# Normalizing two groups of the second batch beside the first batch's products

## The chip, the cores and the metric

The kernel runs on one core of one Trainium2 chip. The metric is the device time of one execution in microseconds (us); lower is better.

## The reference

The input x is 128 samples of 128 nodes with 256 features, adj is 128 matrices of 128x128; everything is float32. Two layers follow each other, each added to its input:

```
h = relu(layernorm(x));  x = x + L0(h, adj)
h = relu(layernorm(x));  x = x + L1(h, adj)
```

L0 computes a convolution branch (a 1x1 convolution, relu, a convolution of 17 taps over the nodes, relu with a skip), a neighbour branch (a 3-component embedding, A = exp(-distance) * adj, and A times a message product), and combines both with h in a GRU cell. L1 is a small graph network: five groups of up to 25 nodes, two graph convolutions each, weighted and added.

## The kernel before

The 128 samples are worked on in 32 groups (q) of 4, and for the convolution in two batches of 16 groups. The 17-tap convolution is done in the frequency domain, with 80 points and 40 frequency steps (f from 0 to NF = 39).

The stages that matter here:

- `stage_a(q)` (L367): loads x of a group into a tile xa, takes mean and variance (`moments`, L261: per group four bn_stats, four bn_aggr and one add on VectorE, then a power on POOL, which is GpSimd), normalizes in place (`normalize`, L273: four tensor_scalar on VectorE), transposes on TensorE into PSUM (ph, L386), copies with relu to hTa on ScalarE, sends hTa to memory for later (L391), multiplies by the 1x1 convolution (pc, L397; its bias add is h, L400), and transforms to frequencies (pf, L408) into the big tile X.
- `stage_b(bat)` (L477): the products of one batch. For each f, two weight planes are loaded ahead (wf, L487, on SP's queue, into one of four buffers), POOL adds two pairs of operands (xs L495 and wf L496), TensorE makes pa and pb (L501), ScalarE copies pb to kk, VectorE combines them to y (L524), and POOL sends y to memory (yd).
- `early(q)` (L632): the neighbour branch of a group, five kinds of TensorE work (pse L580, pm L600, pd L613 with the turn of adj L615, px L626) with VectorE and ScalarE between them (ef, lr, msg, aT, xnmp). It is independent of the products, and is run beside stage_a and stage_b.
- `fold_gates` (L304): loads the gate weights on SP, then combines them in place on POOL (wrz, wn, wh).
- Later, `stage_c` (the inverse transform and the GRU cell) and the second layer, which the change does not touch.

The instructions' order is written by a planner in Python, not by the hardware. Each stage is a generator that emits some instructions and yields (cost, latency): the planner's clock advances by the cost, and this generator is not asked again before the latency has passed. A `Lane` is a list of generators of which up to `ahead` run at once; `Order.run` (L183) always asks the lane with the least work done per weight among those that are ready. A step of no cost raises its lane's account to the least of the others. On the chip each engine then runs its own queue strictly in the order emitted.

In this order, the first batch's stage_a ends and its products run beside `early`; then `take_turn` closes the pool of the products (xw) and opens that of stage_a (ab) in the same memory, and stage_a of groups 16 to 31 starts, three groups ahead, beside `early` and `fold_gates`. Where a tile of the new pool lies on one of the old pool, its first writer waits for that tile's last reader. In stage_a, a group that is not yet loaded is loaded by its own stage, with a planned pause of 6 us for the first group of a batch and 14 us for the others; the following group is loaded too, without a pause. Statistics and normalize follow, with pauses of 3 and 2 us:

```
for n in range(q, min(q + 2, (q // BQ + 1) * BQ)):
    if n not in XA:
        load_xa(n)
        if n == q:
            yield 0.0, 14.0 if q > BQ else 6.0
```

PSUM (the memory that TensorE writes) is divided into three buffers with the tag gat and five with the tag tmp; ph, pc, pf, pb, pse, pm, pd and px all take theirs from tmp.

Of the kernel before, what the change touches and what calls it, by code (L numbers as in the profile page):

```python
# [9 lines left out]
FP = mybir.dt.float32  # L10
# [5 lines left out]
B, N, D = 128, 128, 256  # L16
# [3 lines left out]
P = 128  # L20
# [7 lines left out]
BQ = BG // GB  # L28
# [179 lines left out]
def kernel(ctx: ExitStack, tc: tile.TileContext, x, adj, consts, vecs, w_se, conv1_w,  # L208
# [24 lines left out]
    def c(name):  # L233
        a, b = CAT[name]
        return cst[:, a:b]
# [25 lines left out]
    def moments(src, tag):  # L261

        st = f2.tile([P, 4, 6], FP, tag=tag + "st", name="st", bufs=4)
        mv = f2.tile([P, 4, 2], FP, tag=tag + "mv", name="mv", bufs=4)
        rs = f2.tile([P, 4], FP, tag=tag + "rs", name="rs", bufs=4)
        for t in range(4):
            nc.vector.bn_stats(st[:, t], src[:, t])
            nc.vector.bn_aggr(mv[:, t], st[:, t])
        nc.vector.tensor_scalar(rs, mv[:, :, 1], EPS, None, op0=ALU.add)
        nc.gpsimd.tensor_tensor(rs, rs, c("mhalf")[:, :4], ALU.pow)  # L270
        return mv, rs

    def normalize(dst, src, mv, rs):  # L273
        for t in range(4):
            nc.vector.tensor_scalar(dst[:, t], src[:, t], mv[:, t, 0:1], rs[:, t:t + 1],
                                    op0=ALU.subtract, op1=ALU.mult)
# [27 lines left out]
    def fold_gates():  # L304

        wrz, wn, wh = LATE["wrz"], LATE["wn"], LATE["wh"]
        x_in = w_ih.rearrange("(a k p) o -> k p a o", a=2, k=2)
        for slot, (i, k) in ((0, (0, 0)), (1, (0, 1)), (3, (1, 1)), (4, (1, 0))):  # L310
            nc.sync.dma_start(out=wrz[:, slot, 0],
                              in_=w_hh[k * P:(k + 1) * P, i * D:(i + 1) * D])
            nc.sync.dma_start(out=wrz[:, slot, 1:], in_=x_in[k, :, :, i * D:(i + 1) * D])
            nc.sync.dma_start(out=wn[:, slot],
                              in_=x_in[k, :, :, 2 * D + i * P:2 * D + (i + 1) * P])
            nc.sync.dma_start(out=wh[:, slot, 0], in_=w_hh[k * P:(k + 1) * P,
                                                           2 * D + i * P:2 * D + (i + 1) * P])
            yield 0.0, 8.0
        for w in (wrz, wn, wh):
            for dst, a, b, op in ((6, 0, 4, ALU.subtract), (4, 4, 3, ALU.add),  # L320
                                  (5, 4, 0, ALU.subtract), (2, 1, 5, ALU.subtract)):
                nc.gpsimd.tensor_tensor(w[:, dst], w[:, a], w[:, b], op)
                yield 0.0, 5.0
            nc.gpsimd.tensor_scalar(w[:, 3], w[:, 3], -1.0, None, op0=ALU.mult)
            yield 0.0, 5.0
# [16 lines left out]
    lab, turn = ExitStack(), []  # L342
    xf = lab.enter_context(tc.tile_pool(name="xf", bufs=1, side="right"))
    X = xf.tile([P, 2, F, P], FP, name="X")
    c1w = xf.tile([P, 2, D], FP, name="c1w")
    brow = xf.tile([P, D], FP, name="brow")
    LATE, XA, MOM = {}, {}, {}
    A_DONE, B_DONE, G_DONE, C_DONE = set(), set(), {-1}, set()

    def take_turn(name, bufs, **kw):  # L350
        while turn:
            turn.pop().close()
        turn.append(ExitStack())
        LATE[name] = turn[-1].enter_context(
            tc.tile_pool(name=name, bufs=bufs, side="right", **kw))

    def load_x(t, q):
        for j in range(GB):
            nc.sync.dma_start(out=t[j * WIDE:(j + 1) * WIDE],
                              in_=x[q * GB + j].rearrange("(t n) c -> n t c", n=WIDE))  # L360

    def load_xa(q):
        if q not in XA:
            XA[q] = LATE["ab"].tile([P, 4, D], FP, tag="xa", name=f"xa{q}", bufs=4)
            load_x(XA[q], q)

    def stage_a(q):  # L367
        ab = LATE["ab"]
# [5 lines that stand above are left out]
# [103 lines left out]
    def stage_b(bat):  # L477
        while "wrz" not in LATE:
            yield 0.0, 0.5
        if bat == 0:  # L480
            yield 0.0, 10.0
        WF, xf = {}, LATE["xw"]

        def load_w(f):
            w = WF[f] = xf.tile([P, 2, 3, D], FP, tag="wf", name=f"wf{bat}_{f}", bufs=4)
            for k in range(2):
                nc.sync.dma_start(out=w[:, k, :2], in_=wfd[f::NF + 1, k * P:(k + 1) * P]  # L487
                                  .rearrange("s p o -> p s o"))

        XS = {}  # L490

        def add(f):

            XS[f] = xf.tile([P, 2, P], FP, tag="xs", name=f"xs{bat}_{f}", bufs=2)
            nc.gpsimd.tensor_tensor(XS[f], X[:, :, 2 * f], X[:, :, 2 * f + 1], ALU.add)  # L495
            nc.gpsimd.tensor_tensor(WF[f][:, :, 2], WF[f][:, :, 0], WF[f][:, :, 1], ALU.add)  # L496

        def product(ps, xk, f, s):

            for k in range(2):  # L500
                nc.tensor.matmul(ps, xk(k), WF[f][:, k, s], start=(k == 0), stop=(k == 1))  # L501

        for f in range(3):
            load_w(f)
        yield 0.0, 5.0
        late = None
        for f in range(NF + 1):
            if f + 3 <= NF:
                load_w(f + 3)
            if f < NF:  # L510
                add(f + 1)
            y = xf.tile([P, 2, D], FP, tag="y", name=f"y{bat}_{f}")
            pa = pgat.tile([P, 2, D], FP, tag="gat", name=f"pa{bat}_{f}")
            for s in range(2):
                product(pa[:, s], lambda k: X[:, k, 2 * f + (s if f == 0 else 1 - s)], f, s)
            if f == 0:
                nc.vector.tensor_copy(y, pa)
            else:
                pb = ptmp.tile([P, D], FP, tag="tmp", name=f"pb{bat}_{f}")
                xs = XS.pop(f)  # L520
                product(pb, lambda k: xs[:, k], f, 2)
                kk = xf.tile([P, D], FP, tag="kk", name=f"kk{bat}_{f}", bufs=2)
                nc.scalar.activation(kk, pb, AF.Copy)  # L523
                nc.vector.scalar_tensor_tensor(y, pa, 2.0, kk[:, None].to_broadcast([P, 2, D]),  # L524
                                               op0=ALU.mult, op1=ALU.subtract)
            WF.pop(f)
            if late is not None:
                nc.gpsimd.dma_start(out=yd[bat][:, 2 * f - 2:2 * f], in_=late)
            late = y
            yield 1.7 if f == 0 else 2.6, 1.0  # L530
        nc.gpsimd.dma_start(out=yd[bat][:, F - 2:F], in_=late)
        B_DONE.add(bat)
# [99 lines left out]
    def early(q):  # L632

        while q not in A_DONE:
            yield 0.0, 0.5
        if q not in EN:
            EN[q] = load_n(q)
            yield 0.0, 6.0
        hT, ad = EN.pop(q)
        if q + 1 < NQ and q + 1 in A_DONE:  # L640
            EN[q + 1] = load_n(q + 1)
        xm = LATE["fr"].tile([P, 2, 512], FP, tag="xnmp", name=f"xnmp{q}", bufs=2)
        yield from neighbours(q, hT, ad, xm)
        nc.gpsimd.dma_start(out=xmd[q], in_=xm)
        E_DONE.add(q)
# [447 lines left out]
    order = Order()  # L1093
    take_turn("ab", 2)
    load_xa(0)
    nc.scalar.dma_start(out=c1w, in_=conv1_w.rearrange("(k p) o -> p k o", p=P))
    load_xa(1)
    load_taps(0, nc.sync, nc.gpsimd, nc.scalar)
    load_xa(2)
    fold()  # L1100
    beside = Lane([tap_weights()] + [early(q) for q in range(NQ)])
    gates = Lane([fold_gates()], weight=0.5)
    for bat, (during_a, during_b) in enumerate(((0.66, 0.5), (0.2, 0.65))):
        if bat:
            take_turn("ab", 2, reuse_waits="tile")
        begin = Lane([stage_a(q) for q in range(bat * BQ, (bat + 1) * BQ)], ahead=3)
        beside.weight = during_a
        order.run(begin, beside, *[gates] * bat, until=begin)
        take_turn("xw", 3, reuse_waits="tile")
        products = Lane([stage_b(bat)])  # L1110
        beside.weight = during_b
        order.run(products, beside, *[gates] * bat, until=products)
    turn.pop().close()
    lab.close()
    LATE["co"] = ctx.enter_context(
# [48 lines left out]
```

## Time and profile before

| | us |
|---|---|
| three runs: lowest, median, highest | 2123.21, 2127.03, 2128.71 |
| profiled execution: its own time | 2123.83 |
| its span, first to last instruction | 2122.0 |
| stage_a of the first batch and tap weights | 0 to 209.5 |
| products of the first batch | 209.5 to 369 |
| stage_a of the second batch | 369 to about 536 |
| products of the second batch | about 536 to 703.5 |
| stage_c and the second layer | to 2122 |

The profile is that of one execution. Its engines are PE (TensorE; PEld is its weight load), DVE (VectorE), ACT (ScalarE), POOL (GpSimd) and SP, which here only issues DMAs. A row of a stretch gives its begin and end, its length, then for PE, PEld, DVE, ACT and POOL the busy time and the number of instructions, then the granted TensorE clock (1 is full), the mean busy share of the 16 DMA engines, and GB/s. A row of a timeline gives start, duration, engine, line, operation, tiles and shape; in brackets stands how long the engine was idle just before, and what it waited for. L386 is line 386 of the kernel.

### The profile page before, as it was taken

Reading aid. Unit: us, or ns where it says so; the run is one execution under the profiler, and the core shown is the slowest. Engines: PE = TensorE matmul, PEld = TensorE weight load, DVE = VectorE, ACT = ScalarE, POOL = GpSimd, SP = SyncE. Lnnn points to the kernel's source line nnn. Section 1 sums busy time; section 2 is a strip of 40 time slices with the busy share of each in tenths; the row PEclk is TensorE's granted clock in tenths of the full one; section 3 lists DMA queues with packets and bytes.
Section 4 is the critical chain, followed back from the end, with each engine's and each line's share of the span. In section 5 each row is a group of like instructions: output and inputs, shape, how many; then the busy total and the mean of one; then the engine's idle time right before and its main releaser. Section 6 shows DMA issues by size and latency. Waiting matters only on the chain.

```text
span 2122.0 us, 31227 instructions
## 1 busy us (share of the span) xinstructions
PE 2050.2 (97%) x11316; PEld 1663.0 (78%) x11316; DVE 1239.7 (58%) x2999; ACT 699.6 (33%) x1575; POOL 723.3 (34%) x900
## 2 busy tenths in 40 slices
PE   6999999999999999999999999999999999999998
PEld 4667888788888777788778778878887887878875
DVE  5665444776544566746654655666565655665642
ACT  3554222344222343333223332232223323323333
POOL 2433665331565123512322233223323323233230
PEclk9999999999999999999999999999999999999999
DMA  9997878744787535222223232223232333223121
GB/s 180 270 265 231 261 255 266 217 144 145 256 262 257 171 110 162 61 90 69 69 70 103 77 82 81 78 81 80 75 94 73 81 92 88 78 80 101 26 78 50
DMA packets 187053, 281.68 MB, mean 133 GB/s; under 512 B 20686, under 2 KB 140243, under 8 KB 186899
## 3 DMA queue, kind: packets, MB, share of 16 engines
q1 hardware_dynamic: 156066, 184.81, 30.3%
q0 software_dynamic: 30000, 94.13, 13.9%
q8 instruction: 90, 1.47, 0.3%
q10 hardware_dynamic: 832, 0.74, 0.2%
q14 instruction: 65, 0.52, 0.1%
HBM read 187.34 MB, written 92.27 MB: 132 GB/s over the span
## 4 chain that ended last, share of the span: by engine, by line
PE 84%; DVE 8%; DMA 4%; ACT 2%; issue 1%; POOL 1%; SPq 0%; ACTq 0%; DVEq 0%; POOLq 0%
PE p L708 36%; PE pa L501 7%; PE pm L600 5%; PE ph L1024 5%; PE pz L1033 5%; PE pc L397 4%; PE pb L501 3%; PE px L626 3%; PE pi L673 3%; PE pf L408 2%; PE pg L1067 1%; PE po L848 1%; PE pc L687 1%; DMA xa<-in_x 1%; DMA wfd<-ws 1%; PE py L1007 1%
## 5 line engine op out<-in xcount | busy, mean ns | idle before, releaser
L828 POOL TENSOR_TENSOR d<-hTc,r 128x512 f32<-128x512 f32 x64 | 82.3, 1287 | 318.2 <-ACT r L825 307.8
L857 POOL DMA_DIRECT2D out<-xt x128 | 71.8, 566 | 263.0 <-DVE xt L854 259.0
L501 PE MATMUL pa<-wf,X 128*128 128x256 f32 x640 | 152.4, 381 | 0.0
L524 DVE SCALAR_TENSOR_TENSOR y<-pa,kk 128x512 f32<-128x512 f32 x78 | 53.8, 689 | 147.4 <-ACT kk L523 147.4
L722 ACT ACTIVATE r<-r,brz 128x256 f32<-128x256 f32 x128 | 58.1, 500 | 226.2 <-DVE r L769 198.5
L708 PE MATMUL p<-th,wrz 128*128 128x256 f32 x512 | 131.5, 379 | 0.7 <-ACT u L740 0.7
L708 PE MATMUL p<-tc,wrz 128*128 128x256 f32 x512 | 131.5, 379 | 0.4 <-DVE tc L552 0.4
L708 PE MATMUL p<-tm,wrz 128*128 128x256 f32 x512 | 131.4, 379 | 0.0
L501 PEld LDWEIGHTS pa<-wf,X 128*128 128x128 f32 x640 | 118.1, 190 | 16.4 <-issue 2.2
L397 PE MATMUL pc<-c1w,hTa 128*128 128x256 f32 x512 | 122.8, 386 | 3.5 <-ACT ef L588 2.3
L600 PE MATMUL pm<-wmsg,hT 128*128 128x256 f32 x512 | 123.3, 386 | 0.0
L690 DVE SCALAR_TENSOR_TENSOR xc<-pc,s_bn,hTc 128x256 f32<-128x256 f32 x128 | 53.1, 477 | 115.6 <-PE pc L687 115.6
L1024 PE MATMUL ph<-yz,w 128*128 128x96 f32 (+3 forms) x640 | 114.8, 334 | 4.0 <-DVE ve L795 2.7
L1024 PEld LDWEIGHTS ph<-yz,w 128*128 128x128 f32 x640 | 92.6, 202 | 26.0 <-issue 15.0
L397 PEld LDWEIGHTS pc<-c1w,hTa 128*128 128x128 f32 x512 | 94.3, 192 | 21.8 <-DVE h L400 4.0
L600 PEld LDWEIGHTS pm<-wmsg,hT 128*128 128x128 f32 x512 | 96.9, 192 | 16.3 <-issue 1.4
L1033 PE MATMUL pz<-hh,w 128*128 128x96 f32 (+3 forms) x640 | 108.6, 322 | 0.8 <-ACT hh L1026 0.8
L708 PEld LDWEIGHTS p<-th,wrz 128*128 128x128 f32 x512 | 97.2, 190 | 14.3 <-ACT u L740 1.1
L708 PEld LDWEIGHTS p<-tc,wrz 128*128 128x128 f32 x512 | 97.2, 190 | 14.0 <-DVE tc L552 0.8
L708 PEld LDWEIGHTS p<-tm,wrz 128*128 128x128 f32 x512 | 97.3, 190 | 13.2
L722 ACT ACTIVATE z<-z,brz 128x256 f32<-128x256 f32 x128 | 58.1, 501 | 145.7 <-DVE z L780 90.9
L1033 PEld LDWEIGHTS pz<-hh,w 128*128 128x128 f32 x640 | 87.3, 192 | 19.3 <-ACT hh L1026 1.5
(209 smaller groups left out, 4664.5 us busy)
## 6 DMA issues: line engine op xcount, KB each, us to landing
wf<-wfd SPq DMA_DIRECT2D x160, 256.0 KB, 3.8
wfd<-ws POOLq DMA_DIRECT2D x64, 320.0 KB, 7.2
yd<-y POOLq DMA_DIRECT2D x80, 256.0 KB, 3.9
yt<-yd SPq DMA_DIRECT2D x64, 320.0 KB, 4.5
w<-in_W SPq DMA_DIRECT2D x40, 512.0 KB, 3.6
xa<-in_x SPq DMA_DIRECT2D x128, 128.0 KB, 4.9
hTd<-hTa POOLq DMA_DIRECT2D x32, 512.0 KB, 4.7
hT<-hTd SPq DMA_DIRECT2D x32, 512.0 KB
```

The costliest lines, as they stand in the source:

```text
L397: nc.tensor.matmul(pc[:, i], hT[:, k, (2 * h + i) * N:(2 * h + i + 1) * N], c1w[:, k], start=(k == 0), stop=(k == 1))
L501: nc.tensor.matmul(ps, xk(k), WF[f][:, k, s], start=(k == 0), stop=(k == 1))
L524: nc.vector.scalar_tensor_tensor(y, pa, 2.0, kk[:, None].to_broadcast([P, 2, D]), op0=ALU.mult, op1=ALU.subtract)
L600: nc.tensor.matmul(pm[:, i], hT[:, k, j * N:(j + 1) * N], LATE["wmsg"][:, k], start=(k == 0), stop=(k == 1))
L626: nc.tensor.matmul(px[:, dc, i], msgs[h][:, i, dc * P:(dc + 1) * P], aT[:, 2 * h + i], start=True, stop=True)
L673: nc.tensor.matmul(pi[b * 64:(b + 1) * 64], inv[:F], yt[:, b::2], start=True, stop=True)
L708: nc.tensor.matmul(ps[:, m], w[:, i, k, m * P:(m + 1) * P], factor(i, x, t), start=first and j == 0, stop=last and j == len(n) - 1)
L722: nc.scalar.activation(dst[:, m], src[:, m], AF.Sigmoid, bias=brz[:, b + m:b + m + 1])
L828: nc.gpsimd.tensor_sub(d, hT[:, dc], r[:, dc])
L857: nc.gpsimd.dma_start(out=out[q * GB + j, WIDE:].rearrange("(t n) c -> n t c", n=WIDE), in_=xt[j * WIDE:(j + 1) * WIDE, 1:4])
L1024: nc.tensor.matmul(ph, w1[:, k, m * P:(m + 1) * P], yz[:, k, :, o:o + n], start=(k == 0), stop=(k == 1))
L1033: nc.tensor.matmul(pz, w2[:, g, m, cc * P:(cc + 1) * P], hs[g][:, m], start=(m == 0), stop=(m == 3))
```

## The change

A pool xe with two tiles of its own is opened beside X. While the first batch's products run, a third lane holds one generator, `first_of(1)`: it waits until the products have come to step f = 26, loads x of groups 16 and 17 into the two tiles, and after a planned pause of 14 us takes the moments of the one, normalizes it, and then does the same with the other. stage_a of groups 16 and 17 then finds XA and MOM filled and begins with the transposes. The other groups' tiles still come from the pool ab. In the second batch's products the lanes are as before.

```diff
+    xe = lab.enter_context(tc.tile_pool(name="xe", bufs=1, side="right"))
...
+    def first_of(bat):
+
+        while LATE.get("f", 0) < 26:
+            yield 0.0, 0.5
+        for q in (bat * BQ, bat * BQ + 1):
+            XA[q] = xe.tile([P, 4, D], FP, name=f"xa{q}")
+            load_x(XA[q], q)
+        yield 0.0, 14.0
+        for q in (bat * BQ, bat * BQ + 1):
+            MOM[q] = moments(XA[q], "a")
+            yield 0.0, 4.0
+            normalize(XA[q], XA[q], *MOM[q])
+            yield 0.0, 4.0
...
         for f in range(NF + 1):
+            LATE["f"] = f
...
         beside.weight = during_b
-        order.run(products, beside, *[gates] * bat, until=products)
+        order.run(products, beside, gates if bat else Lane([first_of(1)]), until=products)
```

## The prediction

> **What bounds the kernel now.** I read the page first, then the busy time of each engine by stage, then TensorE's timeline across the seam between the batches, and last the other engines there.
>
> ```profile
> PE 2050.2 (97%) x11316; PEld 1663.0 (78%) x11316; DVE 1239.7 (58%) x2999; ACT 699.6 (33%) x1575; POOL 723.3 (34%) x900
> PE 84%; DVE 8%; DMA 4%; ACT 2%; issue 1%; POOL 1%; SPq 0%; ACTq 0%; DVEq 0%; POOLq 0%
> 209.50:369.00 159.50, 159.50 (x958) 137.99 (x956) 75.94 (x130) 39.12 (x104) 99.13 (x123) 1.00 0.78 256
> 369.00:397.00 28.00, 23.39 (x155) 18.23 (x153) 20.98 (x64) 7.49 (x20) 5.27 (x7) 0.94 0.95 278
> 397.00:420.00 23.00, 23.00 (x148) 20.88 (x148) 17.64 (x50) 10.86 (x25) 7.80 (x8) 1.00 0.45 134
> 420.00:442.00 22.00, 19.10 (x127) 16.53 (x126) 18.15 (x42) 10.83 (x25) 10.83 (x10) 1.00 0.37 120
> ```
>
> TensorE (the first number after each stretch's length) is busy 97% of the span; all its idle time together is 72 us, so a change that removes no TensorE work can only win there. The rows are the first batch's products (209.5 to 369), the seam (369 to 397) and the start of the second batch's stage_a. In the products TensorE never stops and VectorE (the third busy time) works 75.9 of 159.5 us. At the seam TensorE stands still 4.6 us, its clock falls to 0.94, and VectorE works 21.0 of 28 us. The timeline of TensorE shows what it does there:
>
> ```profile
> 371.29 2.05 PE L626 MATMUL px<-aT,msg 128*128 128x128 f32 x16 [0.91 <-DVE aT L618]
> 379.32 0.48 PE L613 MATMUL pd<-lr 32*128 32x128 f32 x2 [1.33 <-DVE msg L603]
> 380.34 2.06 PE L386 MATMUL ph<-cst,xa 128*128 128x128 f32 x8
> 382.20 3.33 PE L626 MATMUL px<-aT,msg 128*128 128x128 f32 x16
> 391.83 1.69 PE L386 MATMUL ph<-cst,xa 128*128 128x128 f32 x8 [0.34 <-PE pm L600]
> 395.84 0.81 PE L408 MATMUL pf<-cst,h 128*128 128x160 f32 x4 [1.78 <-ACT ef L588]
> 396.90 1.35 PE L408 MATMUL pf<-cst,h 128*128 128x160 f32 x8 [0.25 <-DVE msg L603]
> ```
>
> The first transposes of group 16 (ph) start at 380.34, 11 us after the last product; until then TensorE runs `early` work, a filler that it can do anywhere. Idle time understates the loss, since ph goes at the pace of normalize (8 in 1.86 us from start to start; 0.87 where x is ready, 401.67 to 402.54) and px at a slow clock (16 in 3.17 us). So I price 369.29 to 396.90 by start-to-start times in undisturbed stretches: 16 pd 0.88, 8 adj turns 0.98, 32 px 3.56, 32 pse 1.14, 24 pm 5.16, 16 ph 1.74, 16 pc 3.46, 8 pf 1.09: 18.0 us of work in 27.6. **The seam loses 9.6 us**, 0.45% of the time; that is what the change can reach. The next stretch loses nothing. A later one (420 to 442, 2.9 us idle) is another matter:
>
> ```profile
> 420.92 5.20 DVE L275 TENSOR_SCALAR xa<-xa,mv,rs 128x256 f32<-128x256 f32 x4
> ```
>
> Four normalizes, elsewhere 0.40 us each, take 5.20 us while POOL adds wrz (1.83 us each, L322).
>
> **What the Trainium skill says.** "SBUF — State Buffer", section "Who interferes with whom": VectorE in a two-port mode, which tensor_scalar can enter, and GpSimd share a port pair as an exclusive lock, and the loser waits for a whole instruction. The 5.20 us agrees. "DMA: Bandwidth & Descriptors", section "Issuing engines are not separate DMA queues": all DMAs run on the same 16 engines and interleave. The trace agrees in that wf loads land in 4.1 us (median, 300 to 370) at a share near 0.8, and a 256 KB wrz load in 8.8 us at 0.95. "TensorE: Matmul & The Clock Gate", section "What's actually happening": the clock falls after an idle window of about 3.4 us. Here it fell to 0.83 (380 to 390) with no gap over 1.33 us, so I don't count on the page for it.
>
> **The change, part by part.**
>
> 1. Added beside the products: 8 DMAs of 128 KB on SP. first_of polls after step f=26. Steps come every 3.9 us and f=36 began at 352.8, so this is about 314. Price: 8 x 0.43 = 3.4 us of SP, and 1 MB at the 260 GB/s of the stage, 4 us of the DMA engines. Behind them on SP stand the next wf load and the early loads. A wf tile is loaded three steps (11.7 us) ahead of its product and two (7.8 us) ahead of POOL's add, and lands in 4.1 us; if late by 3 to 7 us it delays the add by 0 to 3.5, and pb needs the sum 3 us after the add's usual end. Cost to TensorE: 0 to 3 us, taken as 0. The new pool is written by nothing before, so these loads wait for no tile. More traffic speeds nothing up, so a gain is excluded.
> 2. Added on VectorE in 313 to 367: per group 4 statistics at 0.40, 4 aggregates at 0.18, one add at 0.17, 4 normalizes at 0.40: 4.1 us, 8.2 us for both, into 29 us that it idles there (25.05 of 54 busy). If POOL's adds (xs 0.74, wf 1.27) stretch both normalize blocks to the 5.2 us seen above, 15.4 us: still inside. What is queued behind a block decides: y has two further PSUM buffers and 7 us, msg and lr more. The aT products have little: pd at 331.9, aT done at 333.97, px at 335.43, 1.5 us to spare. A 2.5 us block of moments ahead of aT costs TensorE about 1 us. By the planned times (14.0 after a load at f=26, steps 3.7 apart with a beside step between) the first block falls behind f=30, just ahead of such a pd. The others fall beside px, pse and pm. POOL gets two pows of 1.03 us, as much less later. Cost: 0 to 4 us; I take 0.7.
> 3. Moved away from the seam: the same 8.2 us of VectorE, 2 pows, 8 DMAs. Group 16's and 17's transposes can follow the last product (pm ends about 369.2) at once, and stage_a skips its planned waits of 6, 14, 3 and 2 us. Early work is filler, so the two cycles that stood there are done later where TensorE is full anyway: no gain and no cost by themselves.
> 4. What is late next. (a) PSUM: the tag tmp has five buffers; after ph of group 16 (two), pd wants four, and ph of group 17 two more, each freed through ScalarE and VectorE: about 2 us. (b) stage_a(17) loads group 18, and stage_a(18), started right after it, issues moments(18) with no planned wait: the 14 us pause was only for a group that a stage loads itself. VectorE is one queue; h1 of group 16, msg and xnmp stand behind that wait. Before, group 18's DMAs went out at 367.70, freed by the last pb, and landed in 2.7 us, so by 372.2; VectorE would come to them about 374. No wait, if the tile lies where it did. (c) Group 19's loads went out from 375.47 and landed in up to 7.3 us, by 387; its moments come when group 16 is done, about 383: 0 to 4 us. Together I leave 4 us of loss at the seam (bounds 2 and 13).
> 5. The planner. The new lane keeps `products` from being credited while it waits at its start. Products then lead over beside by more, but each step's pause of 1.0 already admits one beside step, the order that the timeline shows: no change. After the seam about 11 us of early work slides to later, and with it the phases at 703 to 730, where TensorE idles 3.3 of 26.5 us, and POOL's wrz adds against normalize: -2 to +2 us, taken as 0.
>
> **Sum.** 9.6 - 4 - 0.7 = 4.9 us less: the profiled execution's 2123.83 (span 2122.0 and 1.8 around it) becomes 2118.9. It lies 3.2 us under the median of the three runs, 2127.03, and is no different program; from the median I forecast **2122.0 us**. 0.3%, or 6.4 us, is about what a measurement of this kernel can tell from no change, so the forecast lies just inside it.
>
> **Rivals.**
>
> - *Fuller gain.* The filler covers the PSUM turns, loss left 1 to 2 us, and the relieved VectorE also escapes the stretch at 420 (half of 2.9): 8 to 10 us, 2118. For it: 397 to 420 loses nothing at nearly the same mixture. Against: five buffers.
> - *Gain handed back.* The moved filler is missed or bunches at another stage start, or the products lose 3 us: 0 +- 3, 2126. For it: 703 to 730 loses as at the seam.
> - *Slower: moments(18) blocks VectorE.* If group 18's tile lies where group 19's did (375.47), landing by 387, VectorE stands from 374 to 387 with h1 of group 16 behind it. TensorE has transposes, pc and px for about 9 us, until PSUM is full at 383, and then waits out the landing, 2.6 us of moments and the backlog, 9 to 12 us; with 4 us of other loss that is 13 to 16 against 9.6, and with up to 3 us in the products +4 to +9: 2133.5. It decides from a landing after about 384. Against it: group 18 is the first tile of its tag, and the earlier ones were free by 367.7.
> - *The change doesn't do what it says.* The 30 planned us of first_of must fit before the products end: 13 steps remain, 48 us. Excluded.
>
> **How the numbers follow.** Likeliest case 45% (2119 to 2124), fuller gain 25%, handed back 15%, slower 15%. Faster by over 0.3% takes the fuller gain and a third of the likeliest: 0.40; slower takes most of its case: 0.14; the rest 0.46. The range from 2114.5 to 2130 leaves out the far slower half and the best tail.
>
> **What would show it.** Right: ph starts within 2 us of the last product; the products stay 159 to 161 us long; bn_stats of group 18 doesn't wait for its DMA; the seam's TensorE idle falls from 4.6 to under 2 us; `early` ends later. Wrong: DMA xa as the releaser of statistics near 374, px waiting for aT by several us at 330 to 345, wf late for POOL, or a longer idle at 703 to 730.

## The result: slower, and where the profile shows it

| | before, us | after, us |
|---|---|---|
| runs of the comparison: lowest, median, highest (4 each) | 2118.18, 2125.12, 2128.71 | 2146.71, 2151.92, 2152.57 |
| span of the profiled execution | 2122.0 | 2149.4 |

After takes 1.0118 times as long as before, 95% interval 1.0097 to 1.0138. The forecast was 2122.0 (2114.5 to 2130): neither its range nor its sign held. The line numbers of after are 15 or 16 higher than those of before from line 367 on (L626 has become L642, L708 L724); each row has those of its own kernel.

The page of after, row of busy time. TensorE issues the same 11,316 matmuls but is busy 17.5 us longer, and it stands still for 81.7 us where it was 71.8. So most of the 27.4 us that the span has gained is TensorE working slowly, not standing still:

```profile
PE 2067.7 (96%) x11316; PEld 1673.5 (78%) x11316; DVE 1242.3 (58%) x2999; ACT 706.1 (33%) x1579; POOL 722.4 (34%) x900
```

The stretches that the prediction showed, now of after:

```profile
209.50:369.00 159.50, 156.00 (x931) 133.72 (x930) 83.56 (x152) 37.47 (x101) 99.82 (x124) 0.99 0.79 254
369.00:397.00 28.00, 27.37 (x177) 24.37 (x176) 14.61 (x34) 12.03 (x27) 5.50 (x9) 1.00 0.88 262
397.00:420.00 23.00, 20.18 (x114) 17.20 (x112) 14.25 (x47) 7.92 (x17) 3.12 (x4) 0.85 0.52 148
420.00:442.00 22.00, 20.70 (x122) 18.26 (x115) 18.25 (x44) 9.28 (x22) 11.93 (x10) 0.96 0.31 109
```

The products (first row) now contain 3.5 us of idle TensorE where there was none. The seam (second row; in after its first 5 us still belong to the products, which end at 374.3 instead of 367.6) is what was hoped for: idle 0.6 us instead of 4.6, clock 1.00 instead of 0.94. The row after it had lost nothing before; now it idles 2.8 us at a clock of 0.85. The matmul counts in the same 28 and 23 us say so too: 155 and 148 before, 177 and 114 after.

The largest loss is in none of these rows. It lies 480 us later, in stage_c, which the diff does not touch. First before, then after:

```profile
880.00:930.00 50.00, 50.00 (x229) 38.52 (x225) 28.61 (x70) 15.04 (x35) 15.89 (x22) 0.97 0.23 65
```

```profile
880.00:930.00 50.00, 42.27 (x176) 32.60 (x175) 32.55 (x87) 11.82 (x24) 22.50 (x37) 0.83 0.27 72
```

**A measure for the whole run.** Stages shift against each other, so equal times are not equal work. I give each matmul record a price: the mean of the shorter nine tenths of the distances from start to start between neighbours of its kind (same tiles and shape) in before. Lost time of a part is the time it took less the prices of the matmuls in it. It counts idle time and slow clock together. Its own bias shows in the second batch's products, which never stop and "lose" 7.6 to 8.9 us in every kernel. Every "lost" is read from one execution; kernels of one and the same order differ by 1 to 2 us in a part, and by up to 4 us in the first. In us:

| part (ends with) | before | after | difference |
|---|---|---|---|
| up to the first batch's last pb | 82.1 | 88.8 | +6.7 |
| stage_a of the second batch (last pf) | 18.4 | 19.9 | +1.5 |
| products of the second batch | 8.5 | 8.3 | -0.2 |
| to the first matmul of stage_c (pi) | 6.5 | 6.7 | +0.2 |
| stage_c to the second layer's block 0, then block 1 (their pdg) | 10.9, 2.5 | 27.8, 3.9 | +18.3 |
| rest | 73.6 | 74.5 | +0.9 |
| sum | 202.5 | 229.9 | +27.4 |

The sum is the difference of the spans. There are three things to explain: 18.3 us in stage_c, 6.7 us up to the end of the products (0.8 of them before the first product, where nothing was changed), and a stage_a that gained 9 us at its start and kept none of it.

**The 18.3 us.** stage_a of the two groups no longer has its planned pauses for statistics and normalize, and the planner puts one cycle of `early` less beside stage_a and one less beside the products that follow: 16 cycles are done when stage_a ends (17 before), 27 when stage_c starts (29 before). With the loads alone moved, as in a kernel below, 17 and 29 stay. The rest is done beside stage_c, and the second layer's `setup_1` (L880) begins only after all of it (`while len(E_DONE) < NQ: yield 0.0, 1.0`, L881). The last cycle's pse moves from 800.9 to 833.6, and with it pb2, a matmul near the end of `setup_1`, from 851.8 to 876.5. After `setup_1`, `prepare(blk)` (L949) then lets POOL add adjacency rows into b (L961), VectorE sum them to dg (L966), and TensorE multiply both (pa, pdg). This is where it now falls, all engines of after in order of start (start, duration, engine, line, operation, tiles):

```profile
889.07 0.59 PE L724 MATMUL p<-tc,wn 128*128 128x256 f32 x2
...
891.24 0.15 DVE L940 TENSOR_SCALAR rs<-mv 128x1 f32<-128x1 f32 x1
891.54 0.55 POOL L941 TENSOR_TENSOR rs<-rs,cst 128x1 f32<-128x1 f32 x1 [6.14 <-DVE rs L940]
892.07 2.93 POOL L961 TENSOR_TENSOR b<-aj,cst 25x400 f32<-25x400 f32 x8
893.06 0.77 DVE L966 TENSOR_REDUCE dg<-b 25x16 f32<-25x400 f32 x2 [1.67 <-POOL b L961]
...
895.03 0.25 DVE L966 TENSOR_REDUCE dg<-b 25x16 f32<-25x96 f32 x1 [0.26 <-POOL b L961]
895.21 0.40 DVE L823 TENSOR_TENSOR v<-v,p 128x256 f32<-128x256 f32 x1
...
895.66 1.22 PE L724 MATMUL p<-tm,wn 128*128 128x256 f32 x2 [6.00 <-DVE v L823]
896.67 1.06 PE L724 MATMUL p<-tc,wn 128*128 128x256 f32 x2
```

Read the brackets from the bottom up. TensorE stood 6.00 us for v. v (L823) stood in VectorE's queue behind the sums (L966). The sums stood for POOL's b. POOL could not begin b until its power (L941) was done, for which it had waited 6.14 us for VectorE. Every engine was idle in turn. Afterwards two matmuls take 1.06 us where the same form took 0.59 at 889.07: the granted clock is 0.50 from 896 to 900. The Trainium skill, "TensorE: Matmul & The Clock Gate", section "What's actually happening", says that the clock falls after an idle window of about 3.4 us; this gap is longer, and here the trace agrees. In before POOL's b began at 856.0 and the sums at 862.1, and VectorE did not wait for it. Of the 18.3 us, some 13 to 14 lie in the 50 us row shown: 7.7 of idle time and 42.3 at 0.83 instead of 0.97.

**The loss in the products.** TensorE's timeline:

```profile
346.31 1.89 PE L516 MATMUL pa<-wf,X 128*128 128x256 f32 x8
351.54 2.07 PE L516 MATMUL pb<-wf,xs 128*128 128x256 f32 x4 [3.33 <-POOL wf L511]
```

and the other engines in the gap:

```profile
348.22 0.17 DVE L269 TENSOR_SCALAR rs<-mv 128x4 f32<-128x4 f32 x1
348.48 1.03 POOL L270 TENSOR_TENSOR rs<-rs,cst 128x4 f32<-128x4 f32 x1 [3.79 <-DVE rs L269]
349.50 0.72 POOL L510 TENSOR_TENSOR xs<-X 128x256 f32<-128x256 f32 x1
350.19 1.30 POOL L511 TENSOR_TENSOR wf<-wf 128x512 f32<-128x512 f32 x1
```

POOL's power is only 1.03 us long, but it stands in POOL's queue 3.79 us before it may start, because VectorE's statistics come late. The two adds behind it are what pb needs. TensorE stops for 3.33 us and runs the next four matmuls in 2.07 us. Before runs the same form without a wait in half of that:

```profile
350.94 1.03 PE L501 MATMUL pb<-wf,xs 128*128 128x256 f32 x4
```

The granted clock of after there (351.5 to 353.6) is 0.50. By the measure, 340 to 360 loses 5.2 us more than before.

**stage_a.** The transposes do follow the last product with only one pm between, 1.6 us after it:

```profile
374.10 1.89 PE L616 MATMUL pm<-wmsg,hT 128*128 128x256 f32 x8
375.82 1.04 PE L401 MATMUL ph<-cst,xa 128*128 128x128 f32 x8
```

By the measure the seam of after (374 to 394) loses 1.4 us. But the next 20 us lose 8.4, so the 40 us together lose 9.8, against 10.7 in the 40 us of before (364 to 404). In those next 20 us TensorE is idle for 2.8 us, and from 406 to 412 its granted clock is 0.50, though no gap of TensorE from 380 to 412 is longer than 1.75 us. The statistics of groups 19 and 20 run in a row on VectorE there, with msg and h behind them:

```profile
396.78 0.42 DVE L267 BATCH_NORM_STATS2 st<-xa 128x6 f32<-128x256 f32 x1
...
401.55 0.68 DVE L619 TENSOR_TENSOR msg<-pm,bmsg 128x512 f32<-128x512 f32 x1
402.15 0.68 DVE L415 TENSOR_TENSOR h<-pc,brow 128x512 f32<-128x512 f32 x1
...
403.36 1.58 PE L401 MATMUL ph<-cst,xa 128*128 128x128 f32 x8 [1.75 <-ACT msg L621]
```

This pair looked like the cause; splitting it did not bring the loss back.

### The profile page after: what moved, and what is told of

It is laid out like the page before. It is cut to its first block, busy times and chain, and to the rows that moved or that the text cites. A ratio compares the mean times of both kernels' runs of the same rounds, so it can differ in the third digit from the quotient of the medians.

```text
span 2149.4 us, 31213 instructions
## 1 busy us (share of the span) xinstructions
PE 2067.7 (96%) x11316; PEld 1673.5 (78%) x11316; DVE 1242.3 (58%) x2999; ACT 706.1 (33%) x1579; POOL 722.4 (34%) x900
## 4 chain that ended last, share of the span: by engine, by line
PE 52%; DVE 5%; ACT 1%; issue 0%; POOL 0%; POOLq 0%; DVEq 0%
PE p L724 33%; PE ph L1040 4%; PE pz L1049 4%; PE pi L689 3%; PE pg L1083 1%; PE po L864 1%; PE pc L703 1%; PE py L1023 1%; PE pfu L1092 1%; DVE r L773 1%; PE pa L972 1%; DVE th L568 0%; ACT z L738 0%; DVE u L795 0%; DVE z L796 0%; DVE tm L568 0%
## 5 line engine op out<-in xcount | busy, mean ns | idle before, releaser
L873 POOL DMA_DIRECT2D out<-xt x128 | 71.8, 566 | 265.3 <-DVE xt L870 265.1
L724 PE MATMUL p<-tc,wrz 128*128 128x256 f32 x512 | 131.5, 379 | 0.0
L724 PE MATMUL p<-th,wrz 128*128 128x256 f32 x512 | 131.5, 379 | 0.0
L516 PEld LDWEIGHTS pa<-wf,X 128*128 128x128 f32 x640 | 118.0, 190 | 17.2 <-issue 3.0
L724 PE MATMUL p<-tm,wrz 128*128 128x256 f32 x512 | 131.4, 379 | 0.0
L724 PEld LDWEIGHTS p<-tc,wrz 128*128 128x128 f32 x512 | 97.2, 190 | 13.6 <-DVE tc L568 0.4
L724 PEld LDWEIGHTS p<-tm,wrz 128*128 128x128 f32 x512 | 97.3, 190 | 13.2
L724 PEld LDWEIGHTS p<-th,wrz 128*128 128x128 f32 x512 | 97.0, 190 | 13.5 <-issue 0.4
L724 PE MATMUL p<-hTc,wrz 128*128 128x256 f32 x384 | 104.8, 396 | 0.0
```

The lines of the kernel that those rows point to most:

```text
L724: nc.tensor.matmul(ps[:, m], w[:, i, k, m * P:(m + 1) * P], factor(i, x, t), start=first and j == 0, stop=last and j == len(n) - 1)
L873: nc.gpsimd.dma_start(out=out[q * GB + j, WIDE:].rearrange("(t n) c -> n t c", n=WIDE), in_=xt[j * WIDE:(j + 1) * WIDE, 1:4])
```

## The experiments

Each ratio is to runs of the kernel before on the same chip, with its 95% interval. "Lost" is the measure above. The filler's weight in stage_a and in the products is the pair of numbers in `(during_a, during_b)`; the second batch has (0.2, 0.65). In the texts on record, S names the theory that filler which slid behind the products causes most of the loss, Q that POOL's power holds up its adds in the products, W that VectorE's long normalizes (beside POOL's gate adds) cause stage_a's loss, and T that two statistics in a row do. Early x stands for x of groups 16 and 17 loaded and normalized beside the products, late x for before.

### Is the loss in stage_c caused by the filler's place alone?

Undo it in after: a larger weight in stage_a brings the cycles back.

```diff
-(0.2, 0.65)
+(0.32, 0.65)
```

> The changed kernel with the filler's weight in the second batch's stage_a raised from 0.20 to 0.32, so that as many early cycles are done when stage_c starts as in the kernel before (29 instead of 27), and prepare(0) falls at the same place of the same group. Theory S (the bulk of the loss is early work that slid behind the products, so that set-up and preparation of the second layer come at a bad place): about 18 us of the 27 come back, near 2134 us, with TensorE's 6 us wait for v (a VectorE that waits for POOL's b) gone. Rival P (the loss lies in the products and the seam): no change, 2150 to 2153.

2135.91 us, 1.0052 (1.0035 to 1.0069). 29 cycles were done at stage_c's start as in before. Blocks 0 and 1 lost 13.0 and 2.6, so 16.1 of the 18.3 us came back. stage_a lost more, 26.1.

Make it in before, with no x moved: a smaller weight in the products leaves 27 cycles at stage_c's start.

```diff
-(0.2, 0.65)
+(0.2, 0.55)
```

> The kernel before with the filler's weight in the second batch's products lowered from 0.65 to 0.55, and nothing else: 27 early cycles when stage_c starts, and prepare(0) two matmuls after the first pi of group 4, where it falls in the changed kernel. No x is loaded earlier. Theory S: about 18 us slower than before, near 2143. Rival P: the same as before within 4 us.

2139.37 us, 1.0064 (1.0042 to 1.0087). Blocks 0 and 1 lost 28.3 and 3.8, together 32.1 against 31.7 in after. The list of TensorE's waits (us in total, times, longest) shows the same stop. First before, then after, then this kernel, each in 703 to 930, then the one with 0.32 in 700 to 1100:

```profile
PE p L708 <- DVE v L807: 1.1, 2, 0.6
```

```profile
PE p L724 <- DVE v L823: 6.5, 2, 6.0
```

```profile
PE p L708 <- DVE v L807: 6.5, 2, 6.0
```

```profile
PE p L724 <- DVE v L823: 1.2, 2, 0.6
```

So the largest loss does not need early x. It comes when two cycles of filler are done later, and goes when they are not. All the kernels bear this out: in the five that have done 27 cycles when stage_c starts, block 0 loses 23.2 to 28.3 us; in the others, with 29 to 32, at most 17.2.

Leave it late, but give POOL time in after:

```diff
     # prepare(blk), after POOL's adds of b
+    yield 0.0, 7.0
     dg = pool2.tile([NN, SB, NG], FP, tag="dg", name=f"dg{blk}")
```

> The changed kernel with a planned pause of 7 us in prepare between POOL's eight adds of b and VectorE's five sums of it. Theory S, its second half (VectorE stands at the sums until POOL is through, and stage_c's v behind it): the 11 us lost between set-up and pdg of block 0 fall to about 1, and other blocks gain a little: 2138 to 2142. Rival: the wait only moves to the next VectorE instruction of the chain, 2150 to 2153.

2137.67 us, 1.0060 (1.0037 to 1.0083). Block 0 lost 23.2 instead of 27.8, so only a part of its loss is this wait; the longest wait for v fell from 6.0 to 2.1 us. The gain was mostly elsewhere: the rest, with six more such blocks, lost 64.0 instead of 74.5. The same line in before gives this:

> The kernel before with the planned pause of 7 us between POOL's adds of b and VectorE's sums in prepare, and nothing else. If the pause helps every block (theory V: VectorE waits for POOL's b in each of the eight), 8 to 12 us faster than before, near 2116. If it only takes away the bad place that the changed kernel has at block 0 (theory S alone), the same as before within 4 us.

2124.03 us, 0.9993 (0.9983 to 1.0002): the rest lost 69.9 instead of 73.6, but block 0 lost 17.0 instead of 10.9, since there POOL had already been ahead. With the pause from block 1 on:

```diff
+    if blk:
+        yield 0.0, 7.0
```

> The kernel before with the pause of 7 us in prepare for blocks 1 to 7 only; block 0 stays where it is. With the pause for all blocks, block 0 lost 5 us more and the rest of the kernel gained 3. So 3 us below the kernel before, 2121 to 2124; if the gain was chance, the same as before.

2120.25 us, 0.9979 (0.9972 to 0.9986). This helps a little and owes nothing to the change; it is the yardstick for what early x adds later on.

### Which part of first_of costs the products their time?

Only the loads are kept in first_of:

```diff
         yield 0.0, 14.0
-        for q in (bat * BQ, bat * BQ + 1):
-            MOM[q] = moments(XA[q], "a")
-            yield 0.0, 4.0
-            normalize(XA[q], XA[q], *MOM[q])
-            yield 0.0, 4.0
```

> The changed kernel with first_of cut to its loads: x of groups 16 and 17 comes into the two tiles beside the products, statistics and normalize stay in stage_a. The late order (29 early cycles before stage_c, place of prepare(0)) is that of the kernel before. Theory Q with S: the loads cost the products nothing (they end at the time of the kernel before, within 1 us) and the late part costs nothing: 2122 to 2128. Rival D (the loads hold up wf): the products are 3 to 5 us longer, 2130.

2124.56 us, 1.0000 (0.9990 to 1.0010); up to the last pb 81.6 lost against 82.1. The 8 transfers cost nothing that can be measured.

All of it is kept, but POOL's power, taken out of `moments` into `raise_rs`, is issued 4 us later by the plan:

```diff
-            MOM[q] = moments(XA[q], "a")
+            MOM[q] = moments(XA[q], "a", power=False)
             yield 0.0, 4.0
+            raise_rs(MOM[q][1])
+            yield 0.0, 3.0
             normalize(XA[q], XA[q], *MOM[q])
```

> The changed kernel, but in first_of POOL's pow is emitted in a step of its own, 4 planned us after the statistics, and normalize 3 after that. TensorE's order is unchanged. Theory Q (in the products POOL stands at the pow until VectorE has the variance, and its adds for the next step, behind it, come late): the 3.3 us wait of pb for POOL's wf near 351 goes, and with it the slow clock after it, some 5 us: near 2147. Rival D (the 1 MB of x crowds out the loads of wf): the wait stays, 2152.

2144.13 us, 1.0088 (1.0060 to 1.0115). pb no longer waits; 85.3 lost instead of 88.8. Of TensorE's waits, none over 0.2 us is left in 330 to 372. Up to the last pb the seven other kernels with the same edit lost 82.2 to 85.1, but most of that spread arises before the first product. From step 23 of the 39 steps of products to their end the measure is steady: 2.5 us lost in all nine kernels without early statistics, 3.3 in all eight with the later power, and 8.4 to 9.6 in the three with the power in its old place (8.4 in after). So of the 5.9 us that the products of after lose here, 5.1 are the power's place in POOL's queue, and 0.8 all the other added work. VectorE's normalizes are stretched just as at 420 in before (four in 5.30 us at 357.35), and no TensorE wait over 0.2 us follows.

### What sets stage_a's loss?

T first: a pause of 5 us ahead of the second statistics of the pair, in after with the later power (group 20), and in before (group 18).

```diff
         if q not in MOM:
+            if q - BQ in (4,):        # before: (2,)
+                yield 0.0, 5.0
             MOM[q] = moments(XA[q], "a")
```

> The changed kernel with the pow in a step of its own, and a planned pause of 5 us ahead of the statistics of group 20, so that they no longer follow those of group 19 back to back on VectorE. Late order as in the changed kernel. Theory T (the seam's loss was not the late x but two groups' statistics in a row on VectorE; the change moved that pair from groups 17 and 18 to 19 and 20, near 400): the 7 us lost near 400 fall to 2 or less, 2138 to 2141. Rival U (stage_a is short of VectorE as a whole, so the loss turns up elsewhere in stage_a): as with the pow alone, 2142 to 2146.

2142.15 us, 1.0083 (1.0068 to 1.0098). stage_a lost 18.9; with the pair 20.0. No more than runs differ.

> The kernel before with a planned pause of 5 us ahead of the statistics of group 18, so that they no longer follow those of group 17 back to back; no x is moved and the late order is unchanged. Theory T (the pair costs TensorE): stage_a's loss of 18.4 us falls by 4 or more, 2118 to 2122. Rival U: it stays at 18 to 20, 2123 to 2127.

2126.18 us, 1.0003 (0.9995 to 1.0011). stage_a lost 19.0 (18.4). Again nothing for T.

W next: POOL's gate adds are kept out of stage_a in before.

```diff
-        order.run(begin, beside, *[gates] * bat, until=begin)
+        order.run(begin, beside, until=begin)
```

> The kernel before, but fold_gates runs only beside the second batch's products, not beside its stage_a. Without the third lane the planner places four more early cycles in stage_a (21 done at its end, 32 when stage_c starts). Theory W (what stage_a loses after the seam is normalize held up by POOL's adds of wrz): the loss from the last product of the first batch to the last pf, 18.4 us before, falls to 15 or less. Theory S: no early work is left beside stage_c, so the 6.9 us lost there before go. Together 2112 to 2120. Rival U (stage_a loses the same whatever is taken out of it): its loss stays at 18 to 20 us.

2146.25 us, 1.0106 (1.0091 to 1.0121). No normalize is long any more (0.44 us at most), and stage_a lost 32.9, not less. So W does not account for the loss. It is not priced by this run, though: without the gates' lane the planner also has 21 cycles of filler done by the end of stage_a instead of 17, and other things than the normalizes made the stage worse.

The same with early x, the later power and 0.32:

> The changed kernel with the pow in a step of its own, filler weight 0.32, and fold_gates only beside the second batch's products; 32 early cycles when stage_c starts, as in the kernel before without the gates there. If the early x is worth something once VectorE is free of POOL (theory W), stage_a loses 4 us or more less than in that kernel and the time is 2 to 5 us below it. Rival U: stage_a's loss is the same as there within 1.5 us, and the time is 0 to 5 us above it.

2143.99 us, 1.0089 (1.0073 to 1.0105). stage_a lost 23.0. That is 9.9 us less than the kernel just above, with the same lanes and the same 21 cycles, and about the size the seam was priced at. But the filler's weight differs too (0.32 against 0.2), so how much of it early x is worth is not shown. Most was handed back: between blocks 0 and 1 it lost 12.6 instead of 5.6.

### Can everything be had together?

Later power, pair split, 0.32 and the pause in every block, first with the gates beside stage_a, then without them (there with the pause from block 1):

> The changed kernel with all four: pow in a step of its own, pause ahead of the statistics of group 20, filler weight 0.32 in the second batch's stage_a, pause in prepare. If the four causes are separate and add up, the products lose 3 us against before, stage_a gains 3 to 5, the late part stands as in the kernel before with the pause in prepare: between that kernel and 4 us below it, 2112 to 2120. If stage_a loses with weight 0.32 what it lost there before (26 us against 20), 2122 to 2126.

2122.67 us, 0.9992 (0.9982 to 1.0002): the same as before. stage_a lost 19.1, and block 0, with the pause, 16.7.

> The changed kernel with the pow in a step of its own, the pause ahead of the statistics of group 20, filler weight 0.32, fold_gates only beside the second batch's products, and the pause in prepare for blocks 1 to 7. If the gains add up: 3 to 6 us below the kernel before without the gates, near 2110. If the place of prepare(0) (group 3, just before pi) is a bad one as in the changed kernel, 2118 to 2124.

2133.00 us, 1.0037 (1.0023 to 1.0052). stage_a lost 19.3; the time was lost behind it, in block 1 (7.7 instead of 2.5) and in the rest (some 6 us more than before). With the gates, and the pause from block 1:

> The changed kernel with pow in a step of its own, pause ahead of the statistics of group 20, filler weight 0.32, and the pause in prepare for blocks 1 to 7. Late order as in the kernel before with that last pause (2120). With stage_a's loss at 19 as in the earlier run of these mends: 2119 to 2122, no gain over that kernel. If the early x pays: 2114 to 2118.

2119.49 us, 0.9974 (0.9965 to 0.9983); stage_a lost 17.6. The losses in the products and in stage_c are mended but for 1 us, and early x is still worth nothing against the yardstick's 0.9979. The same with late x (before with pair split and pause from block 1) is as fast:

> The kernel before with the pause ahead of the statistics of group 18 and the pause in prepare for blocks 1 to 7. Theory T: 4 us below the kernel with the second pause alone (2120), near 2116. Rival U: 2119 to 2122.

2120.98 us, 0.9978 (0.9968 to 0.9988); stage_a lost 17.9. Next, one number alone is changed, the filler's weight in stage_a:

```diff
-(0.32, 0.65)
+(0.36, 0.65)
```

> As the kernel before it in this list, with filler weight 0.36 instead of 0.32: in the order emitted no two groups' statistics then stand closer than 15 VectorE instructions after group 17's, where 0.32 has one at 11 and one at 13. Late order unchanged. Theory T: stage_a loses 14 to 16 us and the time is 3 to 5 us lower than with 0.32. Rival U: the same within 1.5 us.

2113.56 us, 0.9942 (0.9929 to 0.9954). stage_a lost 12.0, the first time under 17.6. The row of the stretch 369 to 535 of four kernels. Before:

```profile
369.00:535.00 166.00, 158.21 (x1055) 138.97 (x1054) 120.81 (x331) 73.30 (x167) 46.16 (x57) 0.99 0.55 175
```

After:

```profile
369.00:535.00 166.00, 159.74 (x996) 141.98 (x995) 111.17 (x295) 72.42 (x161) 48.59 (x59) 0.97 0.53 166
```

Mended, weight 0.32:

```profile
369.00:535.00 166.00, 158.32 (x1058) 139.28 (x1058) 115.61 (x306) 72.94 (x167) 44.09 (x54) 1.00 0.54 173
```

Mended, weight 0.36:

```profile
369.00:535.00 166.00, 162.60 (x1089) 143.40 (x1089) 116.24 (x313) 74.58 (x173) 47.96 (x58) 1.00 0.57 179
```

Busy time misleads here; the number of matmuls in it is the better sign. After is busy longer than before and got through 996 in 166 us where before got through 1055; the last one got through 1089. Between the two mended kernels, both at a clock of 1.00, idle time tells: 7.7 us at 0.32, 3.4 at 0.36.

Is the pair's split needed? Without it:

> As e15, but without the pause ahead of the statistics of group 20, which then stand right behind group 19's; all else in the order emitted is nearly the same, the late order is the same. If one pair brings the loss back, stage_a loses 17 to 20 us and the time is 2118 to 2121; if a pair costs only what it delays there, 14 to 16 us and 2115 to 2118; if pairs don't matter, as e15, 12 us and 2113.

2113.43 us, 0.9942 (0.9930 to 0.9954); stage_a lost 11.8. So one pair of statistics in a row costs nothing at 0.36, as one split pair had gained nothing at 0.2. Several pairs in one stage were not tested alone: the first kernel with 0.32 began three groups' statistics 9 to 11 VectorE instructions after another's and lost 26.1, the two later ones with 0.32 and the gates began one so and lost 17.6 and 19.1; but in these the power was issued later too.

Does spacing the statistics do it without early x? Before, with the pause from block 1 and 3 us ahead of the statistics of every second group from 18 to 28:

```diff
+            if q - BQ in (2, 4, 6, 8, 10, 12):
+                yield 0.0, 3.0
```

> The kernel before with a planned pause of 3 us ahead of the statistics of groups 18, 20, 22, 24, 26 and 28, which spreads them in the order emitted (13 to 18 VectorE instructions apart but for one pair and one gap), and the pause in prepare for blocks 1 to 7. x comes as in the kernel before; the late order is another (30 early cycles when stage_c starts, prepare(0) four matmuls into group 4), so only stage_a's loss is read. If spacing does it alone, 12 to 15 us against 18.4; if the early x is needed too, 17 to 20.

2126.92 us, 1.0005 (0.9997 to 1.0014); stage_a lost 24.2. No; but this order also has one cycle of filler more done at stage_a's end (18).

The best version is thus after with the power issued later, a weight of 0.36 and the pause from block 1: 11.8 us under before at the median, some 6 to 8 of them beyond the yardstick (by the medians and by the ratios).

## Why the prediction was wrong, step by step

| step of the prediction | forecast | the runs |
|---|---|---|
| 1, loads beside the products | 0 | 0 (loads alone: 1.0000) |
| 2, statistics and powers in the products | 0.7 lost | 5.9 lost: 5.1 by the power's place, 0.8 by the rest |
| seam, first ph after the last product | within 2 us | 1.6 us |
| 4, what is late next | 4 lost of 9.6, 5.6 kept | nothing kept: stage_a lost 1.5 more, no more than runs differ |
| 3 and 5, filler done later | 0 (-2 to +2) | 18.3 lost |

**Steps 3 and 5 failed, and made two thirds of the loss.** "No gain and no cost by themselves" priced the filler by its length. In a static order, however, two cycles of it moved decide where everything that waits for the filler's end falls. The prediction named the phases at 703 to 730, and px's waits for aT in 703 to 930 did grow (from 3.3 to 4.8 us); but it looked only at what the filler meets, not at `setup_1` and `prepare` behind it. The two weight kernels show it from both sides. The sign did not hang on this step alone: without the 18.3 us after would still be some 9 us slower than before, by the products and by a seam of which nothing was kept.

**Step 2 failed in its second half.** The aT products were named as the risk, and px waited for aT only 0.17 us; that part, 0.7 us, was about the 0.8 that stayed with the later power. "POOL gets two pows of 1.03 us, as much less later" counted the power's duration, and not its wait for VectorE, with POOL's adds queued behind it. The bound, 0 to 4 us, was also too low for a gap that halves the clock. The kernel with the power later shows this.

**Step 4 had the right size for the seam and the wrong idea of what it buys.** The 9.6 us priced there agree with the 10.7 that the measure finds, and the seam's first 20 us now lose only 1.4. Loss (a), PSUM turns, and (c) were taken as 4 us; the next 20 us alone took 8.4. (b), statistics of group 18 standing for their DMA, did not come: they ran at 379.81 without a wait. "That is what the change can reach" took stage_a's loss as a sum of places. No kernel with late x lost under 17.9 there; with early x it was 12 in two kernels and 17.6 to 26 in others with the gates' lane, kernels that differ in little but the filler's order. The opening looked at the 72 us of idle time alone for what such a change can do; but it can also lose by slower matmuls, and 17.5 of the 27.4 us are busy time.

**The rivals.** "Gain handed back" named filler that bunches, at a price of 0 to 3 us, a sixth of what it cost, and at other stage starts. The slower rival had the right sign by the wrong mechanism; it would have put the loss at 374 to 387.

**What stays open.** Neither one pair, nor the long normalizes, nor spacing explains why stage_a loses 12 us at one weight and 18 at another, with the same number of cycles done at its end. The traces show only that less is waited for: TensorE's waits for msg (up to 2.3 us at 0.32) and for ef are gone at 0.36, and what is left are waits of up to 0.6 us for hTa and aT. Late x was run with no other weight in stage_a than 0.2, so how the last 6 to 8 us divide between early x and the better filler order is not settled. What is shown is that the combination has them, and that early x without it does not. And in block 0 the reading of the one wait is only in part confirmed: the pause took back 4.6 of its 16.9 us.

## What to carry to other kernels

In a static order, price a moved step also by what is planned after its end and slides with it: find the next place where one engine waits for a second that waits for a third, and ask whether the slide lands there. An instruction that needs another engine's fresh result costs its queue the wait, not its duration; issue it only when its input is old. And when a change opens time for filler, choose the filler's weight again before judging the change: here the same edit, with other orders around it, was 1.2% slower, the same, or 0.6% faster (0.2% of that by the pause in `prepare`, which has nothing to do with it).

## What the hardware showed that I had not expected

- A TensorE gap of 3.33 us was enough for half speed on the next matmuls (four in 2.07 us instead of 1.03), and one of 6.00 us likewise (two in 1.06 instead of 0.59). In before the clock had fallen to 0.83 with no gap over 1.33 us, and in after to 0.50 (406 to 412) with none over 1.75, so one long gap is not the only way there.
- Normalizes stretched by POOL's adds (four in 5.30 us at 357.35 with the later power, elsewhere 0.40 each) were followed by no TensorE wait over 0.2 us in the products, and a stage_a without any lost more, not less, though its filler's order had changed as well.
